# Two graph layers on one core: where the late layers' weights and the filler rows are sent from

## The chip, the core and the metric

The kernel runs on one core of a Trainium2 chip. A core has five engines that each work through their own queue of instructions in order: TensorE (PE, with its weight loads shown as PEld), VectorE (DVE), ScalarE (ACT), GpSimd (POOL) and SyncE (SP). A transfer (DMA) is issued by an instruction in the queue of SyncE, ScalarE or GpSimd. The metric is the device time of one execution in microseconds; lower is better.

## The reference, cut to what matters

Sixteen graphs of 1024 nodes with 64 channels, given as dense 0/1 adjacency matrices, go through two layers. Each layer normalizes, applies a graph network and adds its input back.

```python
def first_network(x, adj, mask, W1, b1, W2, b2):
    # neighbours; of nodes with more than 10, every skip-th edge is removed, both ways
    nb = neigh.sum(-1); skip = where(nb > 10, (nb + 1) // 2, 1)
    rem = neigh & (skip > 1) & (rank % skip == skip - 1) & mask
    nd = adj without (rem | rem.T), with the node itself
    # per node and channel: quantiles 0.25, 0.5, 0.75 over its neighbours' values
    s = sort(where(nd[..., None], x[:, None], inf), axis=2)
    agg = 0.25 * q25(s) + 0.5 * q50(s) + 0.25 * q75(s)
    return (relu((x + agg) @ W1 + b1) @ W2 + b2) * mask

def second_network(x, adj, W1, b1, g1, be1, m1, v1, ..., Wl, bl):
    # three graph convolutions, each with a batch norm of fixed statistics
    x1 = bn(relu(adj @ (x  @ W1) + b1), g1, be1, m1, v1)
    x2 = bn(relu(adj @ (x1 @ W2) + b2), g2, be2, m2, v2)
    x3 = bn(relu(adj @ (x2 @ W3) + b3), g3, be3, m3, v3)
    return relu(concat(x1, x2, x3) @ Wl + bl)

h = maximum(layernorm(x), 0); x = x + first_network(h, adj, mask, ...)
h = maximum(layernorm(x), 0); x = x + second_network(h, adj, ...)
```

## The kernel before

The graphs are handled in eight pairs. Each pair passes three stages.

- `prepare(p)` (L639) makes a pair ready. It loads `x` (L648), normalizes it (L600 to L608), and writes the result to `h_d` (L652) and, in four pieces for each graph, to `rows_d` (L655). Then, for each of the two graphs, `prepare_one` (L765) takes the adjacency in eight tiles of 128 rows. A tile `a` is loaded by SyncE (L775) into one of two buffers; ScalarE makes `edge` from it (L782), VectorE makes `one` (L786), TensorE turns that (L789), and ScalarE stores the turned tile in `edgeT` (L792). When a graph's eight tiles are done, `edgeT` is stored (L797) and its diagonal is cleared (L799). Counting, removing edges, ordering the nodes by degree (`place`, L887) and numbering each node's neighbours follow. Last, the pair's normalized values are loaded again (`h_again`, L695) and split into three parts `hp` (L697 to L700).
- Gathering and sorting. For blocks of nodes of like degree, TensorE collects each node's neighbour values by products with `hp` (L1176), and VectorE runs a sorting network over them (L1092) and sums the quantiles. Nodes of three further blocks are fetched instead by GpSimd, row by row from `rows_d` (L1361). A row number there that stands for "no neighbour" points to one of two filler rows that each graph has at the head of its part of `rows_d`: a row of zeros and a row of a very large value.
- `later` (L1537) runs the rest of the first layer and the second layer for a pair: `first_layer` and `next_layer`. These are the only readers of the weights. They begin while the last pair is being sorted.

Ahead of all that stands a set-up part, which makes constants. GpSimd writes 32 lines `line` by memsets (L528) and sends them into the table `bounds` (L530). ScalarE issues the loads of all weights, biases and batch-norm vectors (helpers `weight`, `column`, `row` and `both`, L536 to L582), and VectorE and ScalarE fold each batch norm into a scale and a shift (L571 to L577). Last, VectorE fills a tile `filler` of two rows (L623, L624), and ScalarE sends it to the sixteen places in `rows_d` (L627). The pool of `filler` is opened after the pool of `line` is closed, and takes the same place in the on-chip memory.

What sets the order of the work: the text of the program gives every instruction its rank and its dependences. When the program is built, each engine's queue is laid out from these ranks and from an estimate of when an instruction is ready, so a queue's order can differ from the text's. On the chip each queue then runs in the order laid. In the main loop over pairs, `weave` mixes steps of the next pair's `prepare` and of the gathers into the sort of the present pair, by hand-set shares (`SHARES`, L33). The first pair has no such cover: `prepare(0)` runs to its end before the first gather.

Of the kernel before, what the change touches and what calls it, by code (L numbers as in the profile page):

```python
# [10 lines left out]
F32 = mybir.dt.float32  # L11
# [13 lines left out]
P = 128  # L25
# [383 lines left out]
def graph_layers_kernel(ctx: ExitStack, tc: tile.TileContext, ins, out: bass.AP):  # L409
# [126 lines left out]
    def weight(name, rows, cols, twice=False):  # L536
        t = const.tile([rows * (1 + twice), cols], F32, name=f"w_{name}")
        for k in range(1 + twice):
            nc.scalar.dma_start(out=t[k * rows : (k + 1) * rows, :], in_=ins[name])
        return t  # L540

    def column(name, rows, twice=False):
        t = const.tile([rows * (1 + twice), 1], F32, name=f"c_{name}")
        for k in range(1 + twice):
            nc.scalar.dma_start(out=t[k * rows : (k + 1) * rows, :], in_=ins[name].rearrange("(p o) -> p o", o=1))
        return t

    def row(name, cols):
        t = const.tile([P, cols], F32, name=f"r_{name}")
        nc.scalar.dma_start(out=t, in_=ins[name].partition_broadcast(P))  # L550
        return t

    def both(t, src):

        nc.vector.memset(t, 0.0)
        for k in range(2):
            half = slice(k * C, (k + 1) * C)
            nc.scalar.dma_start(out=t[half, half], in_=src)


    w1 = weight("L0_gnn_W1", C, HID, True)
    w2 = weight("L0_gnn_W2", HID, C)
    b1 = column("L0_gnn_b1", HID)
    b2 = row("L0_gnn_b2", C)
    layers = []
    for i in (1, 2, 3):
        wl = const.tile([P, P], F32, name=f"wl{i}")
        both(wl, ins[f"L1_gnn_W{i}"])
        bl, g, be, m, v = (column(f"L1_gnn_{k}{i}", C, True) for k in ("b", "g", "be", "m", "v"))
        s = const.tile([P, 1], F32, name=f"bn_s{i}")  # L570
        nc.vector.tensor_scalar(s, v, BN_EPS, None, ALU.add)  # L571
        nc.scalar.activation(s, s, AF.Sqrt)
        nc.vector.reciprocal(s, s)
        nc.vector.tensor_tensor(s, s, g, ALU.mult)

        nc.vector.tensor_tensor(m, m, s, ALU.mult)
        nc.vector.tensor_tensor(be, be, m, ALU.subtract)  # L577
        layers.append((wl, bl, s, be))
    wlast = const.tile([P, 3, P], F32, name="wlast")
    for i in range(3):  # L580
        both(wlast[:, i, :], ins["L1_gnn_Wl"][i * C : (i + 1) * C, :])
    blast = row("L1_gnn_bl", C)  # L582

    biases = {}

# [35 lines left out]
    with tc.tile_pool(name="setup_fill", bufs=1) as setup:  # L621
        filler = setup.tile([2, C], F32, name="filler")
        nc.vector.memset(filler, BIG)  # L623
        nc.vector.memset(filler[:1, :], 0.0)  # L624
        for p in range(NP):
            for x in range(2):
                nc.scalar.dma_start(out=rows_d[p][x * ROWS + ZERO_ROW : x * ROWS + BIG_ROW + 1, :], in_=filler)  # L627

    part_z = {
        MID: const.tile([P, len(TAUS), 1, MW], BF16, name="mid_z"),  # L630
# [8 lines left out]
    def prepare(p, pools):  # L639


        work, keep, ps = pools
        st = Pair()
        st.p = p
        room = work.tile([P, 4, 2, NT, C], F32, tag="stays", name="room")
        xt, h, sq = room[:, 0], room[:, 1], room[:, 2].rearrange("p x t c -> p (x t) c")
        for x in range(2):
            nc.sync.dma_start(out=xt[:, x], in_=rows_of(x_d[2 * p + x]))  # L648
        flat = "p x t c -> p (x t) c"
        layernorm_relu(work, h.rearrange(flat), xt.rearrange(flat), sq, T2)  # L650
        for x in range(2):
            nc.sync.dma_start(out=rows_of(h_d[2 * p + x][:, :]), in_=h[:, x])  # L652
            for t in range(4):
                row0 = x * ROWS + 2 + 256 * t
                nc.sync.dma_start(  # L655
                    out=rows_d[p][row0 : row0 + 256, :].rearrange("(u j) c -> j u c", j=32),
                    in_=h[32 * t : 32 * t + 32, x],
                )
        yield
        st.g = {}  # L660
        st.nvs = keep.tile([P, HELD], BF16, tag="nvs", bufs=2, name="nvs")
        r0 = keep.tile([P, 2, NT, SPLIT], U16, tag="r0", name="r0")
        r1 = keep.tile([P, 2, NT, N - REST], BF16, tag="r1", name="r1")
        st.r = (r0, r1)
        rows = {}
        fetch, find_live = [None] * 2, [None] * 2

        def first_rows():
            rows[0] = fetch[0]()

        for x in range(2):
            fetch[x], find_live[x] = yield from prepare_one(st, x, pools, first_rows if x else None)
        rows[1] = fetch[1]()
        yield
        listed = work.tile([P, 2 * len(NODES) - 1, 256], F32, tag="stays", name="listed")
        st.nodes_nv = keep.tile([P, 2 * len(NODES) - 1], F32, tag="nodes_nv", bufs=2, name="nodes_nv")
        for x in range(2):
            find_live[x] = yield from find_live[x](rows[x], listed)
        yield from list_rows(st, listed, pools)
        for x in range(2):  # L680
            find_live[x]()
            yield


        st.z = keep.tile([P, len(TAUS), HELD], BF16, tag="z", name="z")
        half = work.tile([P, HELD], F32, tag="a", bufs=2, name="half")
        nc.vector.tensor_scalar(half, st.nvs, 0.498, MAGIC, ALU.mult, ALU.add)
        nc.vector.tensor_scalar(half, half, MAGIC, None, ALU.subtract)
        for q, (tau, _) in enumerate(TAUS):
            nc.vector.scalar_tensor_tensor(st.z[:, q, :], st.nvs, -tau, half, ALU.mult, ALU.add)  # L690
        yield

        h = work.tile([P, 2, NT, C], F32, tag="a", bufs=2, name="h_again")
        for x in range(2):
            nc.sync.dma_start(out=h[:, x], in_=rows_of(h_d[2 * p + x][:, :]))  # L695
        st.hp = keep.tile([P, 3, 2, NT, C], BF16, tag="hp", name="hp")
        nc.scalar.copy(st.hp[:, 0], h)  # L697
        nc.vector.tensor_tensor(h, h, st.hp[:, 0], ALU.subtract)
        nc.scalar.copy(st.hp[:, 1], h)
        nc.vector.tensor_tensor(st.hp[:, 2], h, st.hp[:, 1], ALU.subtract)  # L700
        yield
        return st
# [743 lines left out]
    def first_layer(pools, xt, h, agg, mask):  # L1446


        one, ps = pools
        X = xt.shape[2]  # L1450
        nc.vector.tensor_tensor(agg, agg, h, ALU.add)  # L1451
        oT = channels_first(pools, agg, "chan")
        yield
        for x in range(X):
            rows = slice(x * C, (x + 1) * C)
            hT = one.tile([HID, N], F32, tag="hT", name="hT")
            for hf in range(NH):
                sl = slice(hf * HALF, (hf + 1) * HALF)
                pm = ps.tile([HID, HALF], F32, tag="mm", name="pm1")
                nc.tensor.matmul(out=pm, lhsT=w1[rows, :], rhs=oT[rows, sl], start=True, stop=True)  # L1460
                nc.scalar.activation(hT[:, sl], pm, AF.Relu, bias=b1)
            py = ps.tile([P, NT, C], F32, tag="mm", name="py")
            for t in range(NT):
                nc.tensor.matmul(out=py[:, t, :], lhsT=hT[:, t * P : (t + 1) * P], rhs=w2, start=True, stop=True)  # L1464
            nc.vector.tensor_tensor(h[:, :, x, :], py, b2[:, None, :].to_broadcast([P, NT, C]), ALU.add)
            yield
        nc.vector.tensor_tensor(h, h, mask[:, :, :, None].to_broadcast([P, NT, X, C]), ALU.mult)
        nc.vector.tensor_tensor(xt, xt, h, ALU.add)
        flat = "p t x c -> p (t x) c"
        layernorm_relu(one, agg.rearrange(flat), xt.rearrange(flat), h.rearrange(flat), NT * X)  # L1470
        yield
        return channels_first(pools, agg, "chan")

    def next_layer(pools, graphs, adjT, x2, cur):
# [4 lines left out]
        XC = X * C  # L1479
        small = adjT[0].dtype == F8  # L1480
        xs = []
        for i, (wl, bl, s, be) in enumerate(layers):

            if small:
                xw = [one.tile([P, NT, XC], BF16, tag=f"xw{k}", name=f"xw{k}") for k in range(3)]
# [33 lines left out]
        for hf in range(NH):  # L1519
            ts = slice(4 * hf, 4 * hf + 4)  # L1520
            pf = ps.tile([P, 4, X, C], F32, tag="mm", name="pf")
            for t in range(4):
                sl = slice((4 * hf + t) * P, (4 * hf + t + 1) * P)
                for i, xT in enumerate(xs):
                    nc.tensor.matmul(  # L1525
                        out=pf[:, t].rearrange("p x c -> p (x c)"), lhsT=xT[:, sl], rhs=wlast[:XC, i, :XC],
                        start=(i == 0), stop=(i == 2),
                    )
            nc.vector.tensor_tensor(
                res[:, ts], pf, blast[:, None, None, :].to_broadcast([P, 4, X, C]), ALU.add  # L1530
            )
        nc.vector.scalar_tensor_tensor(res, res, 0.0, x2, ALU.max, ALU.add)  # L1532
        for x in range(X):
# [210 lines left out]
    with ExitStack() as stack:  # L1744
# [6 lines left out]
        with ExitStack() as inner:  # L1751
# [3 lines left out]
            )  # L1755
            ahead = Steps(prepare(0, early))
            ahead.rest()
            sts = [ahead.result]
            jobs = iter(NODE_ORDER)

# [131 lines left out]
```

## Time and profile before

| what | value |
|---|---|
| time of the kernel, median of 3 runs | 2845.74 us (2841.83 to 2846.65) |
| the profiled execution's own time | 2855.05 us |
| its span, first to last instruction | 2853.2 us |
| mean granted TensorE clock | 0.869 |
| busy: PE, DVE, ACT, POOL | 75%, 79%, 58%, 48% of the span |
| DMA queues: SyncE's, GpSimd's, ScalarE's | 131.39, 62.23 and 8.09 MB |

The page of the profile gives shares over the whole span, the span in 40 slices of 71.3 us, and the costliest groups of instructions. In a timeline line, the first number is the start, the second the duration, both in us; "ACTq" and "SPq" stand for the queue of an engine when it issues a transfer, and the bracket at the end gives how long the engine stood idle before and what ended that. In a line of one source line's instructions, the three durations are least, median and largest in ns. Line numbers such as L627 are those of the kernel before.

### The profile page before, as it was taken

To read this page: it belongs to the slowest core of one execution; us is meant where nothing else is said; L and a number is where in the kernel's file an instruction comes from. 1 tells how busy PE (TensorE), PEld (TensorE's weight loads), DVE (VectorE), ACT (ScalarE), POOL (GpSimd) and SP (SyncE) were. 2 spreads that over 40 slices of the span, in tenths; PEclk is the share of its full clock that TensorE was granted. 3 is DMA by queue.
4 is the path that set the end of the run, shared out by engine and by line. 5 is a ranking of instruction groups with operands and counts; after the bars stand their busy time and mean duration, and the time that the engine had idled before them with its cause. 6 is when DMAs were issued, how large, how long until landed. Compare 5 with 4: busy or idle time off the path is not lost. (4 is left out here: it accounts for less than half of the span.)

```text
span 2853.2 us, 54558 instructions
## 1 busy us (share of the span) xinstructions
PE 2127.4 (75%) x21226; PEld 1374.2 (48%) x21226; DVE 2259.9 (79%) x5356; ACT 1657.8 (58%) x3324; POOL 1358.7 (48%) x1155
## 2 busy tenths in 40 slices
PE   1567986897798699779855986997588496448768
PEld 0344563564455365545523553665355363234445
DVE  3117999889899989989999999989688486647843
ACT  2686788678677858867773777687423141122222
POOL 5115363475526416443734274175646748862220
PEclk9788997998899799789878997998798798778989
DMA  3303222322422323142431222322310351221221
GB/s 96 109 30 98 80 88 65 104 80 58 107 72 86 81 91 91 46 110 68 98 65 45 82 86 73 112 75 61 80 21 19 74 82 51 42 56 39 48 61 46
DMA packets 261035, 205.27 MB, mean 72 GB/s; under 512 B 217120, under 2 KB 217248, under 8 KB 256672
## 3 DMA queue, kind: packets, MB, share of 16 engines
q1 hardware_dynamic: 165120, 131.39, 15.5%
q0 software_dynamic: 39680, 62.23, 9.1%
q10 hardware_dynamic: 55968, 8.09, 2.1%
q8 instruction: 168, 2.75, 0.4%
q14 instruction: 99, 0.81, 0.1%
HBM read 148.82 MB, written 52.75 MB: 71 GB/s over the span
## 5 line engine op out<-in xcount | busy, mean ns | idle before, releaser
L1361 POOL DMA_INDIRECT g_nodes<-rows_d,rows_listed x744 | 979.2, 1316 | 952.5 <-DVE prod L1104 276.2
L1176 PE MATMUL pg<-s,hp 128*64 128x496 fp8e4 (+5 forms) x8064 | 747.0, 337 | 134.9 <-ACT hp L697 56.1
L1176 PEld LDWEIGHTS <-hp 128*64 128x64 bf16 x8064 | 450.2, 113 | 376.9 <-ACT hp L697 67.2
L1509 PE MATMUL pg<-adjT,xw 128*64 128x512 fp8e4 x2304 | 282.5, 394 | 24.6 <-ACT xw L1498 11.4
L895 POOL DMA_INDIRECT live_d<-edge,place x128 | 178.7, 1396 | 191.1 <-DVE place L887 154.9
L1151 DVE TENSOR_SCALAR s<-r 128x3200 uint16<-128x3200 uint16 (+2 forms) x192 | 199.6, 1049 | 56.9 <-PE pg L1176 56.8
L1554 POOL DMA_INDIRECT agg<-agg_d,place x128 | 134.8, 1053 | 196.4 <-DMA agg_d<-agg_nodes 118.0
L1509 PEld LDWEIGHTS <-xw 128*64 128x64 bf16 x2304 | 135.4, 113 | 154.1 <-issue 22.8
L782 ACT ACTIVATE edge<-a 128x1024 fp8e4<-128x1024 uint32 x128 | 135.8, 1062 | 105.1 <-DMA a<-in_adj 87.2
L1180 ACT ACTIVATE g<-pg 128x400 f32<-128x400 f32 (+3 forms) x168 | 84.3, 502 | 191.1 <-PE pg L1176 161.3
L1092 DVE TENSOR_TENSOR t<-g 128x800 f32<-128x800 f32 (+9 forms) x184 | 168.0, 926 | 5.4 <-ACT g L1180 3.4
L884 ACT ACTIVATE stays<-keys,minus 128x1024 fp8e4<-128x1024 f32 x128 | 143.6, 1122 | 41.7 <-PE keys L876 40.5
L865 ACT ACTIVATE edge<-q,bias 128x1024 fp8e4<-128x1024 f32 x128 | 142.2, 1112 | 41.6 <-PE q L860 41.6
L838 ACT ACTIVATE stays<-cs,back 128x1024 f16<-128x1024 f32 x128 | 139.1, 1114 | 41.5 <-DVE look L819 19.8
L789 PE MATMUL ptE<-ident_h,one 128*128 128x128 bf16 x1024 | 83.4, 232 | 106.1 <-DVE one L786 58.0
L1092 DVE TENSOR_TENSOR g<-t 128x992 f32<-128x992 f32 (+7 forms) x176 | 160.0, 934 | 2.4
L1451 DVE TENSOR_TENSOR agg<-agg,h_late 128x1024 f32<-128x1024 f32 x8 | 9.8, 1224 | 184.1 <-DMA agg<-agg_d,place 184.1
L930 PE MATMUL pt<-ident_h,lp 128*128 128x128 bf16 x1024 | 107.7, 276 | 60.7 <-ACT liveT L933 33.2
L1247 PE MATMUL pg<-s,hp 128*64 128x384 bf16 (+14 forms) x1872 | 149.1, 301 | 2.8 <-DVE s L1216 2.7
L792 ACT ACTIVATE edgeT<-ptE 128x1024 fp8e4<-128x1024 f32 x128 | 130.8, 1033 | 19.9 <-PE ptE L789 19.6
L1513 ACT ACTIVATE xT<-pg,c_L_gnn_b 128x512 f32<-128x512 f32 x48 | 32.9, 686 | 183.9 <-PE pg L1509 175.3
L786 DVE TENSOR_SCALAR one<-a 128x1024 fp8e4<-128x1024 f32 x128 | 88.5, 696 | 55.6 <-DMA a<-in_adj 45.3
(253 smaller groups left out, 5043.3 us busy)
## 6 DMA issues: line engine op xcount, KB each, us to landing
a<-in_adj SPq DMA_DIRECT2D x128, 512.0 KB
adjT_d<-edgeT SPq DMA_DIRECT2D x16, 1024.0 KB
lp<-live_d POOLq DMA_DIRECT2D x32, 512.0 KB
adjT<-adjT_d SPq DMA_DIRECT2D x16, 1024.0 KB
g_nodes<-rows_d,rows_listed POOLq DMA_INDIRECT x744
room<-in_x SPq DMA_DIRECT2D x16, 256.0 KB
h_d<-room SPq DMA_DIRECT2D x16, 256.0 KB
rows_d<-room SPq DMA_DIRECT2D x64, 64.0 KB
```

The costliest lines, as they stand in the source:

```text
L782: nc.scalar.activation(edge[:, t, :], a[:, :].bitcast(U32), AF.Sign, accum_out=found[:, 0, b, t : t + 1], saturate=False)
L838: nc.scalar.activation(stays[:, t, :], cs, AF.Abs, bias=back[:, t : t + 1], scale=2.0)
L865: nc.scalar.activation(edge[:, t, :], q, AF.Relu, bias=bias(-2.0), accum_out=nv[:, t : t + 1], saturate=False)
L884: nc.scalar.activation(junk, keys, AF.Sign, bias=minus[:, t : t + 1], accum_out=above[:, t : t + 1], saturate=False)
L895: sent = nc.gpsimd.indirect_dma_start(out=live_d[b][:, :], out_offset=bass.IndirectOffsetOnAxis(ap=place[:, b, t : t + 1], axis=0), in_=ed ...
L1092: sorted_by[0] = nc.vector.tensor_tensor(view(bufs, o, n1, n2), view(bufs, a, n1, n2), view(bufs, b, n1, n2), ALU.max if op else ALU.min)
L1151: nc.vector.tensor_scalar(s[:, j, :, us, :], st.r[0][:, :, us, j0:j1], abs(k - 3), 0x0808, ALU.logical_shift_right if k > 3 else ALU.logic ...
L1176: summed = nc.tensor.matmul(out=pg[x * C : (x + 1) * C, those, :], lhsT=st.hp[:, part, x, u, :], rhs=picked, start=(i == 0 and part == 0), ...
L1247: summed = nc.tensor.matmul(out=pg[x * C : (x + 1) * C, ks, w0:], lhsT=st.hp[:, part, x, u, :], rhs=s[:, ks, x, u, w0:], start=(whole and ...
L1361: asked = nc.gpsimd.indirect_dma_start(out=g[:, k, a * C : (a + 1) * C], out_offset=None, in_=rows_d[st.p][:, :], in_offset=bass.IndirectO ...
L1509: nc.tensor.matmul(out=pg[cs, :], lhsT=part[:, u, cs], rhs=adjT[x][:, u, sl], start=(u == 0 and k == 0), stop=(u == NT - 1 and k == len(xw ...
L1554: nc.gpsimd.indirect_dma_start(out=agg[:, t, x, :], out_offset=None, in_=agg_d[b][:, :], in_offset=bass.IndirectOffsetOnAxis(ap=place[:, b ...
```

## The change

The loads of weights move from ScalarE to SyncE. They are wrapped in a function `load_weights`, called once after `prepare(0)` has been written out, and each load is ordered behind the latest `h_again` load on SyncE, which at that moment is the first pair's. The order is one of the queue alone: nothing waits for the `h_again` data. The batch-norm steps move into the same function. Their readers take them from an object `weights`. The sixteen sends of filler rows move from ScalarE's queue to GpSimd's. The helper `both` is renamed `blocks_of`.

```diff
     def weight(name, rows, cols, twice=False):
         t = const.tile([rows * (1 + twice), cols], F32, name=f"w_{name}")
         for k in range(1 + twice):
-            nc.scalar.dma_start(out=t[k * rows : (k + 1) * rows, :], in_=ins[name])
+            load_one(t[k * rows : (k + 1) * rows, :], ins[name])
         return t
...
-    w1 = weight("L0_gnn_W1", C, HID, True)
-    w2 = weight("L0_gnn_W2", HID, C)
-    b1 = column("L0_gnn_b1", HID)
-    b2 = row("L0_gnn_b2", C)
-    layers = []
-    for i in (1, 2, 3):
...
+    read_last = [None]
+
+    def load_one(to, source):
+
+        load = nc.sync.dma_start(out=to, in_=source)
+        tc.add_manual_dep(
+            load.ins, read_last[0].ins.name,
+            mybir.DependencyInfo(mybir.DependencyClass.NoSync, mybir.DependencyReason.SCHED_ONLY),
+            reason="weights are wanted late",
+        )
...
+    def load_weights():
+
+        w = weights
+        w.w1 = weight("L0_gnn_W1", C, HID, True)
+        w.w2 = weight("L0_gnn_W2", HID, C)
+        w.b1 = column("L0_gnn_b1", HID)
+        w.b2 = row("L0_gnn_b2", C)
+        w.layers = []
+        for i in (1, 2, 3):
+            wl = const.tile([P, P], F32, name=f"wl{i}")
+            blocks_of(wl, ins[f"L1_gnn_W{i}"])
+            bl, g, be, m, v = (column(f"L1_gnn_{k}{i}", C, True) for k in ("b", "g", "be", "m", "v"))
+            s = const.tile([P, 1], F32, name=f"bn_s{i}")
+            nc.vector.tensor_scalar(s, v, BN_EPS, None, ALU.add)
+            nc.scalar.activation(s, s, AF.Sqrt)
...
+            w.layers.append((wl, bl, s, be))
+        w.wlast = const.tile([P, 3, P], F32, name="wlast")
+        for i in range(3):
+            blocks_of(w.wlast[:, i, :], ins["L1_gnn_Wl"][i * C : (i + 1) * C, :])
+        w.blast = row("L1_gnn_bl", C)
...
-                nc.scalar.dma_start(out=rows_d[p][x * ROWS + ZERO_ROW : x * ROWS + BIG_ROW + 1, :], in_=filler)
+                nc.gpsimd.dma_start(out=rows_d[p][x * ROWS + ZERO_ROW : x * ROWS + BIG_ROW + 1, :], in_=filler)
...
         for x in range(2):
-            nc.sync.dma_start(out=h[:, x], in_=rows_of(h_d[2 * p + x][:, :]))
+            read_last[0] = nc.sync.dma_start(out=h[:, x], in_=rows_of(h_d[2 * p + x][:, :]))
...
             ahead = Steps(prepare(0, early))
             ahead.rest()
+            load_weights()
             sts = [ahead.result]
```

More of the change, by code (lines that the diff above doesn't have):

```diff
@@ L544, in column @@
         for k in range(1 + twice):
-            nc.scalar.dma_start(out=t[k * rows : (k + 1) * rows, :], in_=ins[name].rearrange("(p o) -> p o", o=1))
+            load_one(t[k * rows : (k + 1) * rows, :], ins[name].rearrange("(p o) -> p o", o=1))
         return t
@@ L549, in row, with blocks_of @@
         t = const.tile([P, cols], F32, name=f"r_{name}")
-        nc.scalar.dma_start(out=t, in_=ins[name].partition_broadcast(P))
+        load_one(t, ins[name].partition_broadcast(P))
         return t
-    def both(t, src):
+    def blocks_of(t, src):
         nc.vector.memset(t, 0.0)
@@ L557, in both @@
             half = slice(k * C, (k + 1) * C)
-            nc.scalar.dma_start(out=t[half, half], in_=src)
-    w1 = weight("L0_gnn_W1", C, HID, True)
-    w2 = weight("L0_gnn_W2", HID, C)
-    b1 = column("L0_gnn_b1", HID)
-    b2 = row("L0_gnn_b2", C)
-    layers = []
-    for i in (1, 2, 3):
[L567 to L582, printed above, removed]
+            load_one(t[half, half], src)
+    read_last = [None]
[6 more added lines that the diff above has]
+        )
@@ new lines, in graph_layers_kernel @@
+    class Weights:
+        pass
+    weights = Weights()
+    def load_weights():
[12 more added lines that the diff above has]
+            nc.scalar.activation(s, s, AF.Sqrt)
+            nc.vector.reciprocal(s, s)
+            nc.vector.tensor_tensor(s, s, g, ALU.mult)
+            nc.vector.tensor_tensor(m, m, s, ALU.mult)
+            nc.vector.tensor_tensor(be, be, m, ALU.subtract)
+            w.layers.append((wl, bl, s, be))
[3 more added lines that the diff above has]
+        w.blast = row("L1_gnn_bl", C)
@@ L1459, in first_layer @@
                 pm = ps.tile([HID, HALF], F32, tag="mm", name="pm1")
-                nc.tensor.matmul(out=pm, lhsT=w1[rows, :], rhs=oT[rows, sl], start=True, stop=True)
-                nc.scalar.activation(hT[:, sl], pm, AF.Relu, bias=b1)
+                nc.tensor.matmul(out=pm, lhsT=weights.w1[rows, :], rhs=oT[rows, sl], start=True, stop=True)
+                nc.scalar.activation(hT[:, sl], pm, AF.Relu, bias=weights.b1)
             py = ps.tile([P, NT, C], F32, tag="mm", name="py")
             for t in range(NT):
-                nc.tensor.matmul(out=py[:, t, :], lhsT=hT[:, t * P : (t + 1) * P], rhs=w2, start=True, stop=True)
-            nc.vector.tensor_tensor(h[:, :, x, :], py, b2[:, None, :].to_broadcast([P, NT, C]), ALU.add)
+                nc.tensor.matmul(out=py[:, t, :], lhsT=hT[:, t * P : (t + 1) * P], rhs=weights.w2, start=True, stop=True)
+            nc.vector.tensor_tensor(h[:, :, x, :], py, weights.b2[:, None, :].to_broadcast([P, NT, C]), ALU.add)
             yield
@@ L1481, in next_layer @@
         xs = []
-        for i, (wl, bl, s, be) in enumerate(layers):
+        for i, (wl, bl, s, be) in enumerate(weights.layers):
             if small:
@@ L1525, in next_layer @@
                     nc.tensor.matmul(
-                        out=pf[:, t].rearrange("p x c -> p (x c)"), lhsT=xT[:, sl], rhs=wlast[:XC, i, :XC],
+                        out=pf[:, t].rearrange("p x c -> p (x c)"), lhsT=xT[:, sl], rhs=weights.wlast[:XC, i, :XC],
                         start=(i == 0), stop=(i == 2),
@@ L1529, in next_layer @@
             nc.vector.tensor_tensor(
-                res[:, ts], pf, blast[:, None, None, :].to_broadcast([P, 4, X, C]), ALU.add
+                res[:, ts], pf, weights.blast[:, None, None, :].to_broadcast([P, 4, X, C]), ALU.add
             )
```

## The prediction

> **What bounds the kernel now.** I read the page first, then busy time by stretch over the first 330 us, then the waits of the first 80 us, then the timeline there, and last the durations of single DMA issues. On the page, one digit is a fortieth of the span (71.3 us):
>
> ```profile
> DVE  3117999889899989989999999989688486647843
> ACT  2686788678677858867773777687423141122222
> ```
>
> VectorE (DVE) is nearly full from the fifth slice to the 28th: sorting sets the pace there. In the first 230 us it is nearly empty, because nothing can be sorted before the first pair of graphs is prepared. That stretch is a chain with nothing beside it, so a microsecond saved in it should reach the end whole. All that the change touches stands in this chain or just behind it. Busy time by stretch (first the stretch, its length, then PE, PEld, DVE, ACT, POOL with counts, granted clock, DMA share, GB/s):
>
> ```profile
> 0.00:32.30 32.30, 1.89 (x16) 1.60 (x16) 15.44 (x192) 1.89 (x4) 21.71 (x51) 1.00 0.27 60
> 32.30:44.05 11.75, 2.07 (x16) 1.54 (x16) 4.08 (x5) 9.86 (x18) 9.29 (x25) 1.00 0.73 179
> 44.05:61.10 17.05, 1.89 (x16) 1.62 (x16) 1.46 (x4) 0.00 (x0) 8.60 (x47) 1.00 0.24 66
> 61.10:72.50 11.40, 2.07 (x16) 1.64 (x17) 2.08 (x3) 9.64 (x18) 0.00 (x0) 1.00 0.55 184
> 228.00:262.00 34.00, 26.69 (x318) 17.82 (x320) 19.52 (x23) 24.75 (x65) 26.69 (x25) 0.81 0.58 148
> ```
>
> ScalarE (ACT) does two bursts of four adjacency tiles in 11.75 and 11.40 us, and before each it stands still: 32.3 us with 1.89 busy, and 17.05 us with nothing. The timeline says why:
>
> ```profile
> 31.66 0.59 ACTq L550 DMA_DIRECT2D r_L_gnn_bl<-in_L_gnn_bl  x1
> 33.26 1.04 ACT L782 ACTIVATE edge<-a 128x1024 fp8e4<-128x1024 uint32 x1
> 54.05 0.48 POOL L530 DMA_DIRECT2D bounds<-line  x1 [0.29 <-POOL line L528]
> 55.66 0.11 DVE L623 MEMSET filler<- 2x64 f32 x1 [13.86 <-DMA bounds<-line]
> 56.03 5.05 ACTq L627 DMA_DIRECT2D rows_d<-filler  x16
> 61.13 1.06 ACT L782 ACTIVATE edge<-a 128x1024 fp8e4<-128x1024 uint32 x1 [17.08 <-DMA rows_d<-filler]
> 77.02 0.42 DVE L799 TENSOR_TENSOR edgeT<-edgeT,off_diag 128x256 int32<-128x256 int32 x1 [2.91 <-DMA adjT_d<-edgeT]
> ```
>
> The first stop is the issue of weights up to 32.3. The second has two owners. The filler tile lies where the lines of `bounds` lay, so its memset waits for GpSimd's last line (54.05 and its landing); VectorE stands 13.86 us at it; and ScalarE stands behind 16 filler DMAs that wait for it, then needs 5.05 us to issue them.
>
> **The change part by part.**
>
> *Weights off ScalarE.* 48 DMAs leave its queue (3 of `w_`, 31 columns, 12 half blocks, 2 broadcast rows). One issue:
>
> ```profile
> L545 ACTq DMA_DIRECT2D c_L_gnn_v<-in_L_gnn_v x6: 607/609/612, 9.2 to 27.1; - x6
> L1283 ACTq DMA_DIRECT2D agg_d<-o x112: 308/343/2842, 369.3 to 2600.8; - x112
> L1407 SPq DMA_DIRECT2D agg_d<-agg_nodes x32: 326/388/1597, 328.1 to 2732.9; - x32
> ```
>
> 48 x 0.607 = 29.1 us, nearly all of the first stop. A rule of the Trainium skill speaks against a gain (page "DMA: Bandwidth & Descriptors", section "Issuing engines are not separate DMA queues"): issuing from several engines saves only the time of the issue, usually small beside the transfer. By the rule this part is worth about 0. By the row an issue is 0.607 us for at most 32 KB, and 48 of them stand ahead of the chain's first activation. I go by the row. Without them tile 0, asked for at 5.79, can be taken about 3.6 us later (a tile asked for at 34.42 was taken at 37.99): at 9.4 instead of 33.26. Two tiles come before the normalization, whose own chain (L600 to L608, six VectorE steps and two ScalarE steps, some 7 us) then runs beside the tiles. Eight tiles at 2.5 us, plus 6.4 us in which SyncE writes `h_d` and `rows_d` (37.17 to 43.59) instead of asking for tiles, end near 9.4 + 20 + 6.4 = 36 us; before it was 71.3.
>
> *Filler to GpSimd.* Its issue of a small DMA is 0.48 us (L530), so 16 x 0.48 = 7.7 us, from 56 to 64. GpSimd has nothing from 54.5 to 123.7, and its first reader of the rows is at 227.7: cost nothing, and 7.7 us if that cover were gone. ScalarE no longer waits. The memset stays, though, and still waits for the last line at about 55.7: the lines are GpSimd's own work (82 memsets, 23.6 us, and 32 issues, 15.8 us), which nothing here shortens. What is late next is therefore VectorE, which takes its queue in order: all that is put behind the memset waits to 55.7. Where it is put decides the gain. Queues follow an order made when the program is built, from estimated readiness and not from the text (`one`, L786, ran at 15.75 ahead of L576 at 17.27, written far earlier). Before, the memset was put after the fourth tile, 8.8 to 13.7 us after ScalarE's start at 32.3. ScalarE's start moves some 23 us earlier, so the same moment is 32 to 37 us after the new start: all eight `one` (the last near 33, 24 us after the start) come first, and L799, which waits for the store of the eighth (5.5 us, from 71.5 to 77.0), comes behind. L799 then runs at 55.8 instead of 77.0: **gain 21**. Ends: the memset ahead of the fifth `one` as before gives 5.6 (the fifth and sixth tiles' buffers free at 56.6 instead of 62.2); a memset that holds nothing gives 77.0 - 42 = 35. I take 21, by the order as worked out.
>
> *Weights onto SyncE.* They are put behind the last `h_again` of the first pair. What stands there:
>
> ```profile
> 227.46 0.99 SPq L695 DMA_DIRECT2D h_again<-h_d  x2
> 232.00 0.34 SPq L775 DMA_DIRECT2D a<-in_adj  x1
> 236.16 0.69 DVE L786 TENSOR_SCALAR one<-a 128x1024 fp8e4<-128x1024 f32 x1
> 236.76 1.22 DVE L700 TENSOR_TENSOR hp<-h_again,hp 128x1024 bf16<-128x1024 f32 x1
> 242.17 47.96 SPq L775 DMA_DIRECT2D a<-in_adj  x9
> ```
>
> On SyncE these 48 shapes have no row. Bounds: 0.33 (its tile loads), 15.8 us in all, and 0.607 as on ScalarE, 29.1. The like stores above show SyncE no faster than ScalarE (388 against 343 ns), so 29. All being ready at once and earlier in the text than the second pair, they go ahead of its tiles: a second-pair tile asked for at 232.0 is asked for at 257.6 (times of before), behind it ten `h_d` and `rows_d` writes, then the rest. It can be taken at 261, 25 us late. But the eight `one` of that graph were spread from 236 to 288 by the weaving (SyncE once waited 25.9 us for one of them); from 261, at 2.5 us each and 6.4 for the writes, they end at 287. If the queues are laid with the late loads in mind, almost nothing is lost. The batch-norm steps come along: 15 of VectorE at 0.15 (2.3 us), 3 roots of ScalarE at 0.2, and six memsets. VectorE has 14.5 us and ScalarE 9 us idle in 228 to 262, so they cost 0 if the weights arrive when the queue expects them. Before, VectorE waited 10.0 us in all for `c_v`, mostly with nothing to do, but the first 1.57 us with memsets behind it: an issue takes longer than the order assumed. Such waits now stand before the first gather. I bound the part by 0 and 25 and take **3**. The weights' readers come after 2000 us.
>
> Sum: -21 + 3 = **-18 us**: 2855.05 (the profiled execution; its span 2853.2) becomes 2837. That execution was 9.3 us above the median of 2845.74; the difference is carried over to the median: **2828 us**.
>
> **The rivals.**
>
> *The filler keeps its place (little happens).* If the memset again stands before the fifth `one`, the start gains 5.6 and pays 3: 2843. For it: the order is not in the diff, and 13.86 us of waiting shows that it misjudged the lines once. Against it: eight tiles would be ready well before the moment that it was given. This is also the case in which the change does not free the start as it says.
>
> *The filler falls far back.* If it stands behind L820 or among L839, the chain gains 29 to 35; with 2 or 3 paid, 2813 to 2818. For it: VectorE has little to do there and the order may be late rather than early.
>
> *SyncE's burst holds VectorE (slower).* If the second pair's first `one` keeps its place just before L700, VectorE waits for a tile 25 us late; L700 makes the third part of `hp`, which every gather of the first block reads, so TensorE, and the first sort, wait too: +25. It outweighs the start as soon as that gains less than 25. With a start gain of 14, midway between 5.6 and 21, it gives +11: 2857. For it: the trace has exactly this order, and the row of 29 us. Against it: the loads' lateness is known when the order is made, and the `one` can simply move behind.
>
> **How the numbers follow.** Forecast 0.50 (own range 2818 to 2837), filler far back 0.16, filler in place 0.14, slower 0.20. About 0.2% (5.7 us) is what a measurement of this kernel can tell from no change. The first two are faster beyond it: 0.66; the third lies within it: 0.14; the last is slower: 0.20. The range reaches from 2808, below the far-back case, to 2854, which leaves out the larger half of the slower one.
>
> **What would show it.** ScalarE's first L782 near 9 to 12 us and no stop behind filler; a memset L623 still at about 55.7, with the eighth `one` before and L799 right after it; 16 filler issues of GpSimd between 56 and 64; the first gather (L1176, 233.7 before) near 213; 48 issues of SyncE over 26 to 29 us behind L695; the second pair's `one` starting some 25 us after them with VectorE waiting under 5 us for a tile. Wrong if fewer than six `one` run before the memset, if VectorE or ScalarE waits over 10 us for weights or the second pair's tile, or if the first gather's lead is gone by the first sort's end (293.4 before).

## The result and the profile after

The changed kernel took 2827.78 us (median of 7 runs, 2820.77 to 2834.53) against 2845.74 of the kernel before (7 runs, 2840.51 to 2851.97) on the same chip: ratio 0.9937, 95% interval 0.9918 to 0.9956, which is 18.0 us. The forecast was 2828.0. In a later group of runs, where the changed kernel was measured again beside the last experiments, the ratio was 0.9904 (0.9874 to 0.9934). The profiled execution took 2820.77 us, with a span of 2819.0 us against 2853.2. These two spans differ by 34.2 us, more than the kernels do: 2820.77 is the lowest of its kernel's seven runs, and the profiled 2855.05 of before lies above all seven of its own. So below, places in the first 480 us are compared, not spans. In lines below, numbers such as L805 are those of the changed kernel; they lie 19 or 20 above those of before (L786 has become L805, L623 L642, L799 L818, L819, which makes `look`, L838, L838 L857, L1176 L1195, L627 L646).

The two engine rows of the page, in slices of 70.5 us:

```profile
DVE  3137998999999899989999999999688486647943
ACT  4795877678587768868673777687423141122222
```

ScalarE's first slice has gone from 2 to 4, and VectorE's third (141 to 211 us) from 1 to 3: more of the first pair's preparation and the start of its sort have come forward. From the fourth slice on the rows are nearly those of before. Three of the prediction's stretches (first the stretch and its length, then PE, PEld, DVE, ACT, POOL with counts, clock, DMA share, GB/s):

```profile
0.00:32.30 32.30, 4.99 (x40) 3.94 (x40) 19.15 (x184) 14.55 (x23) 20.41 (x46) 1.00 0.55 147
44.05:61.10 17.05, 4.58 (x37) 2.19 (x37) 1.21 (x9) 3.37 (x7) 12.43 (x58) 1.00 0.23 74
228.00:262.00 34.00, 30.87 (x385) 21.07 (x383) 27.87 (x42) 13.56 (x29) 22.66 (x18) 0.95 0.53 137
```

ScalarE now has 14.55 us of work in the first 32.3 us (1.89 before), and the DMA engines are at 0.55 instead of 0.27. The second of these stretches is still almost empty on every engine but GpSimd: a stop is left there. In the last stretch VectorE does 27.87 us instead of 19.52, because the first pair's sort has begun earlier. The timeline of the start:

```profile
0.76 1.28 ACT L801 ACT_TABLE_LOAD   x1 [0.76 <-PEq L1896]
7.05 1.06 ACT L801 ACTIVATE edge<-a 128x1024 fp8e4<-128x1024 uint32 x1 [5.01 <-DMA a<-in_adj]
37.48 0.69 DVE L805 TENSOR_SCALAR one<-a 128x1024 fp8e4<-128x1024 f32 x1 [1.61 <-DMA a<-in_adj]
46.19 0.42 DVE L818 TENSOR_TENSOR edgeT<-edgeT,off_diag 128x256 int32<-128x256 int32 x1 [2.34 <-DMA adjT_d<-edgeT]
58.48 0.49 POOL L530 DMA_DIRECT2D bounds<-line  x1 [0.29 <-POOL line L528]
60.15 0.11 DVE L642 MEMSET filler<- 2x64 f32 x1 [13.53 <-DMA bounds<-line]
60.37 0.10 DVE L827 COPY nb<-nbp 128x8 f32<-128x8 f32 x1
60.73 8.15 POOL L646 DMA_DIRECT2D rows_d<-filler  x16 [1.76 <-DVE act L831]
61.34 2.20 ACT L857 ACTIVATE stays<-cs,back 128x1024 f16<-128x1024 f32 x2 [10.66 <-DVE look L838]
211.21 0.88 PE L1195 MATMUL pg<-s,hp 128*64 128x400 fp8e4 x4 [9.95 <-DVE ln_var L624]
```

ScalarE takes the first tile at 7.05 instead of 33.26, the eighth `one` runs at 37.48 (68.49 before), and L818 at 46.19 instead of 77.02. VectorE then stands 13.53 us at the memset of the filler, which still waits for GpSimd's last line. ScalarE stands 10.66 us behind that, for `look`. The first `stays` (L857, the first step behind the counting) starts at 61.34; before it was 83.37. The first gather starts at 211.21 instead of 233.66. The two lines of the kernel before:

```profile
83.37 1.11 ACT L838 ACTIVATE stays<-cs,back 128x1024 f16<-128x1024 f32 x1 [1.20 <-PE cs L834]
233.66 0.88 PE L1176 MATMUL pg<-s,hp 128*64 128x400 fp8e4 x4 [10.30 <-ACT hp L697]
```

SyncE's queue behind the first pair:

```profile
205.01 0.99 SPq L714 DMA_DIRECT2D h_again<-h_d  x2
206.06 1.92 SPq L565 DMA_DIRECT2D w_L_gnn_W<-in_L_gnn_W  x3
...
237.23 0.58 SPq L565 DMA_DIRECT2D r_L_gnn_bl<-in_L_gnn_bl  x1
244.57 26.90 SPq L794 DMA_DIRECT2D a<-in_adj  x10
```

The 48 weights take SyncE from 206.06 to 237.81, 31.8 us. The second pair's `h_d` and `rows_d` follow, and its tiles come from 244.57 on. Its first `one` runs at 250.83 (before: 236.16).

### The profile page after: what moved, and what is told of

Same layout as the page of the kernel before. It is cut to its first block, busy times and chain, and to the rows that moved or that the text cites. A ratio compares the mean times of both kernels' runs of the same rounds, so it can differ in the third digit from the quotient of the medians.

```text
span 2819.0 us, 54552 instructions
## 1 busy us (share of the span) xinstructions
PE 2124.0 (75%) x21226; PEld 1366.3 (48%) x21226; DVE 2260.5 (80%) x5356; ACT 1660.1 (59%) x3325; POOL 1359.1 (48%) x1171
## 5 line engine op out<-in xcount | busy, mean ns | idle before, releaser
L1380 POOL DMA_INDIRECT g_nodes<-rows_d,rows_listed x744 | 968.6, 1302 | 951.7 <-DVE prod L1123 282.6
L1195 PE MATMUL pg<-s,hp 128*64 128x496 fp8e4 (+5 forms) x8064 | 742.2, 335 | 128.9 <-ACT hp L716 47.4
L1195 PEld LDWEIGHTS <-hp 128*64 128x64 bf16 x8064 | 445.1, 113 | 370.4 <-ACT hp L716 67.5
L857 ACT ACTIVATE stays<-cs,back 128x1024 f16<-128x1024 f32 x128 | 138.8, 1114 | 47.3 <-DVE look L838 28.7
L805 DVE TENSOR_SCALAR one<-a 128x1024 fp8e4<-128x1024 f32 x128 | 89.5, 704 | 53.9 <-DMA a<-in_adj 42.6
```

The lines of the kernel that those rows point to most:

```text
L857: nc.scalar.activation(stays[:, t, :], cs, AF.Abs, bias=back[:, t : t + 1], scale=2.0)
L1195: summed = nc.tensor.matmul(out=pg[x * C : (x + 1) * C, those, :], lhsT=st.hp[:, part, x, u, :], rhs=picked, start=(i == 0 and part == 0), ...
L1380: asked = nc.gpsimd.indirect_dma_start(out=g[:, k, a * C : (a + 1) * C], out_offset=None, in_=rows_d[st.p][:, :], in_offset=bass.IndirectO ...
```

## The experiments

The variants were run in two groups, each beside the kernel before on one chip. Its median was 2853.59 us beside the first three variants of the table and after_filler_own_place, and 2846.56 beside the other four; the row of the changed kernel is the comparison above. So across the groups only ratios compare. Where an expectation names a time, it reckons from the 2845.74 of the first comparison, and its difference is what counts. This table has the places in the profiles that the verdicts rest on, in us; each comes from one execution:

| kernel | first stays | first gather | second pair's first place | second gather | ratio (95%) |
|---|---|---|---|---|---|
| before | 83.37 | 233.66 | 351.95 | 479.49 | 1 |
| filler_by_GpSimd_alone | 76.22 | 226.86 | 349.15 | 476.69 | 0.9971 (0.9952 to 0.9990) |
| before_filler_own_place | 75.27 | 225.70 | 347.89 | 474.86 | 0.9982 (0.9961 to 1.0004) |
| weights_late_filler_by_ScalarE | 69.28 | 221.69 | 342.65 | 473.58 | 0.9948 (0.9923 to 0.9972) |
| the changed kernel | 61.34 | 211.21 | 331.12 | 458.41 | 0.9937 (0.9918 to 0.9956) |
| after_unchanged | 61.68 | 212.16 | 332.51 | 459.29 | 0.9904 (0.9874 to 0.9934) |
| weights_behind_last_pair | 61.22 | 212.63 | 330.82 | 456.73 | 0.9924 (0.9898 to 0.9951) |
| weights_burst_doubled | 61.25 | 211.40 | 357.56 | 477.65 | 0.9979 (0.9959 to 0.9999) |
| after_filler_own_place | 49.39 | 200.69 | 320.72 | 448.65 | 0.9895 (0.9865 to 0.9926) |
| weights_last_filler_own_place | 48.57 | 199.39 | 318.17 | 447.20 | 0.9880 (0.9846 to 0.9915) |

The row after_unchanged is the changed kernel once more: two executions of one program differ by 0.3 to 1.4 us at these places. The second gather is the start of the second pair's sort. Each variant's queues are laid out anew, so the order of other instructions can differ, too, as it does for after_filler_own_place below.

**Weights moved, filler still sent by ScalarE** (weights_late_filler_by_ScalarE), from the changed kernel:

```diff
-                nc.gpsimd.dma_start(out=rows_d[p][...], in_=filler)
+                nc.scalar.dma_start(out=rows_d[p][...], in_=filler)
```

> The changed kernel, but the filler rows are again sent by ScalarE. The order of VectorE and SyncE is that of the changed kernel. Theory (what holds the start is VectorE's wait at the filler memset, about 60.2 us, and the sender costs its issue and what stands behind it): ScalarE waits for the memset too, sends until about 65.5, and only then makes the sums that VectorE's next step needs; the first stays activation comes at about 67.9 instead of 61.3: 6.5 us slower than the changed kernel, 2834, 11 to 12 faster than before. Rival 1 (the weights alone are the whole gain): 0 to 1 us beside the changed kernel, 2828. Rival 2 (the sender was as much as the weights): the 17 us stop of ScalarE is back, 2845.

Measured: 2836.89 us, 0.9948. The first gather is 12.0 us earlier than before, 10.5 later than with the filler on GpSimd. The timeline says why:

```profile
60.27 0.11 DVE L642 MEMSET filler<- 2x64 f32 x1 [13.38 <-DMA bounds<-line]
60.63 5.02 ACTq L646 DMA_DIRECT2D rows_d<-filler  x16
66.02 1.01 ACT L781 CAST sums<-tot 128x1024 bf16<-128x1024 f32 x1 [21.67 <-DMA rows_d<-filler]
67.50 0.17 DVE L827 COPY nb<-nbp 128x8 f32<-128x8 f32 x1 [6.94 <-PE nbp L823]
```

ScalarE stands 21.67 us, with the sends ahead of `sums` in its queue; TensorE's counting and VectorE's `nb` wait behind it. The first `stays` comes at 69.28 (expected 67.9), 7.9 us later than in the changed kernel. The long stop of ScalarE is back, as the second rival has it, but it costs less than its length, because VectorE is held at the memset until about 60.2 in both kernels. Moving the weights alone gives about half of the start: 12.0 of 22.5 us at the first gather. At the second gather 5.9 of 21.1 are left; what takes the rest was not traced. In whole times, the intervals of this run and of the changed kernel overlap.

**Only the filler moved** (filler_by_GpSimd_alone), from the kernel before:

```diff
-                nc.scalar.dma_start(out=rows_d[p][...], in_=filler)
+                nc.gpsimd.dma_start(out=rows_d[p][...], in_=filler)
```

> The kernel before, with only the sender of the filler rows changed to GpSimd; the order of VectorE, TensorE and SyncE is that of before. Theory: VectorE still stands at the memset to 55.7 ahead of the fifth tile; only the 5.05 us of issue go: 5 to 6 us faster than before, 2840. Rival 2 (the sender was the stop): the 17 us go, 2829. Rival 1 (weights are all): 0, 2846.

Measured: 2843.41 us, 0.9971, which is 8.3 us (interval 2.9 to 13.7; expected 5 to 6). The first gather gains 6.8 us, of which 2.8 is left at the second gather. The memset stays where it was, at 54.85 after 13.41 us of waiting, and VectorE's next `one` with it. ScalarE no longer stops for the sends: it takes two more tiles at 47.11 and 48.40, where before the next came at 61.13, but the weights still hold its first tile. So the parts alone are worth 12.0 and 6.8 at the first gather, and together 22.5: each leaves a part of the other's stop standing.

**The filler in a place of its own** (after_filler_own_place and before_filler_own_place): the tile comes from a pool that shares no space with `line`, so the memset has nothing to wait for. The same edit on each kernel:

```diff
-        filler = setup.tile([2, C], F32, name="filler")
+        filler = const.tile([2, C], F32, name="filler")
```

> The changed kernel, with the filler tile in a place of its own, so that its memset waits for no line. Theory (the memset's wait is what limits the changed kernel's start): VectorE's copy of the neighbour counts follows the sums at about 50 instead of 60.4, the first stays activation at about 51 instead of 61.3: 10 us faster than the changed kernel, about 2817. Rival 3 (the adjacency loads, or the second graph's tiles on ScalarE, bind next): less than 4 us faster, 2824 to 2828.

> The kernel before, with only the filler tile in a place of its own; weights and filler rows are still sent by ScalarE. Theory: the sends follow the weights at once and take 5 us, the 17.05 us stop goes, so the chain gains 12: 2834. Rival 2 (ScalarE's sending is what costs, the place does not matter): 0 to 2 us, 2844 to 2846.

Measured: 2820.38 us, 0.9895, on the changed kernel; 2848.01 us, 0.9982, on the kernel before. The first did what was expected:

```profile
6.70 0.11 DVE L642 MEMSET filler<- 2x64 f32 x1
42.46 0.43 DVE L818 TENSOR_TENSOR edgeT<-edgeT,off_diag 128x256 int32<-128x256 int32 x1 [1.88 <-DMA adjT_d<-edgeT]
```

The first `stays` runs 12.0 us earlier than in the changed kernel, of which 9.8 is left at the second gather. Not all of the 12.0 is the memset: L818 itself ran 3.7 us earlier (42.46 against 46.19), since SyncE asked for six tiles and not four ahead of its writes of `h_d` and `rows_d`, and the eighth turned tile was stored at 36.77 instead of 40.44. From L818 to the first `stays` it took 6.9 us instead of 15.2, and these 8.2 us are the memset's stop. The second missed its expectation of 2834: by the ratio it gains 5.1 us, and its interval, 0.9961 to 1.0004, does not exclude that it gains nothing. The memset ran early (14.11), but the sends moved, too:

```profile
14.11 0.11 DVE L623 MEMSET filler<- 2x64 f32 x1
32.28 5.88 ACTq L627 DMA_DIRECT2D rows_d<-filler  x16
39.17 1.04 ACT L782 ACTIVATE edge<-a 128x1024 fp8e4<-128x1024 uint32 x1
```

Now they stand right behind the weights (whose last issue ends at 32.24) and ahead of the first tile, which ScalarE takes at 39.17 instead of 33.26. It gained 8.1 us at the first `stays`, where the 17 us stop, less 5 us for the sends, had been expected to give 12. The sends cost 5.9 us ahead of the first tile, and where the stop had been ScalarE now stands 3.4 us for the load of the fifth tile (at 53.96).

**The burst of weights put elsewhere** (weights_behind_last_pair): `load_weights()` is called when the last pair has been prepared.

```diff
             ahead.rest()
-            load_weights()
...
+                if p == NP - 2:
+                    load_weights()
```

> The weights' 48 loads are issued by SyncE only behind the last pair's preparation instead of behind the first's. The theory, that the burst behind the first pair costs about 3 us net: second pair's first 'one' again ahead of the first gather, first block's aggregation at about 271 instead of 273.7, time 2 to 3 us under the changed kernel's (ratio about 0.992). Rival, the burst is fully hidden: same time within 1 us. Rival, the burst holds VectorE: 8 us or more under.

Measured: 2826.55 us, 0.9924, against 0.9904 of the changed kernel beside it. The expected gain of 2 to 3 us isn't seen in the time, which is 5.1 us longer, with overlapping intervals. In the profile it is there, if one counts from the first gather of the same execution: the first block's aggregation, the end of the first sort, starts 59.6 us behind it without the burst (272.24 against 212.63; in the kernel before 59.7), and 62.5 and 63.0 us behind it in the two profiles with the burst. So the burst costs about 3 us there. The second pair's tiles show how the rest was absorbed. Their first `one` ran at 215.1 without the burst and at 250.8 with it, but the first `stays` of that pair started at almost one time. In the timeline of weights_behind_last_pair:

```profile
283.01 2.12 ACT L857 ACTIVATE stays<-cs,back 128x1024 f16<-128x1024 f32 x2 [3.56 <-DVE look L838]
```

In that of the changed kernel:

```profile
285.06 2.10 ACT L857 ACTIVATE stays<-cs,back 128x1024 f16<-128x1024 f32 x2
```

Without the burst, the `one` of that graph's eight tiles are spread from 215 to 267, and three of them run before VectorE's first sorting step; with it all eight are packed between the sorting steps from 250.8 to 270.7. So a burst of 31.8 us moves the `stays` by 2.1 us, or by 3.5 counted from the first gather.

**The burst doubled** (weights_burst_doubled):

```diff
+            twin = const.tile([P, 24], F32, name="twin")
+            for k in range(48):
+                load_one(twin[k % 2 * C : k % 2 * C + C, k // 2 : k // 2 + 1], ins["L1_gnn_v1"]...)
```

> 48 further small loads (64 partitions by one number, into a tile that nobody reads) are issued by SyncE right behind the 48 weights, which makes the burst about 61 us long. Theory, hidden mostly by the work on tiles already there: second pair's first 'one' about 29 us later (near 280), time 3 to 10 us above the changed kernel's. Rival, free: 0 to 2 us. Rival, SyncE's burst holds VectorE one for one: 29 us above.

Measured: 2842.64 us, 0.9979, which is 21.2 us above the changed kernel of its group, with intervals that don't meet. The theory's 3 to 10 is refuted, and neither rival's number fits. The added loads took 32.62 us of SyncE. Of its timeline, with the second pair's first `stays`:

```profile
238.49 32.62 SPq L565 DMA_DIRECT2D twin<-in_L_gnn_v  x48
276.76 24.30 SPq L794 DMA_DIRECT2D a<-in_adj  x10
315.05 2.12 ACT L857 ACTIVATE stays<-cs,back 128x1024 f16<-128x1024 f32 x2 [0.30 <-DVE look L838]
```

The second pair's first `stays` moved by 30.0 us (from 285.06 in the changed kernel), its first `place` by 26.4 and the second gather by 19.2. VectorE was not held one for one at the tile (it stood 4.34 us for the first, at 280.79): the first block's aggregation of the first pair was even earlier (266.95 against 273.74), as no `one` now runs ahead of it. It lost work later, 6.0 us from 270 to 300 us, around the late tiles, and 7.6 us from 340 to 370. Busy time in the latter stretch of the changed kernel (columns as above):

```profile
340.00:370.00 30.00, 29.09 (x348) 19.27 (x346) 26.11 (x74) 23.42 (x42) 23.70 (x17) 1.00 0.26 83
```

and with the burst doubled:

```profile
340.00:370.00 30.00, 24.99 (x301) 17.71 (x303) 18.49 (x56) 27.52 (x57) 19.45 (x18) 0.89 0.50 150
```

VectorE's work falls from 26.11 to 18.49 us there, with ScalarE nearly full (27.52 of 30 us) and the DMA engines at 0.50 instead of 0.26: the second pair's tiles come in this stretch now (six `one` instead of one). Which of its waits holds the sort is not separated. So the first 31.8 us of burst moved the second pair by 2.1, the next 32.6 by 30.0: the cover of this place is just about used up by the weights themselves.

**The changed kernel unchanged**, as the baseline of this group:

> The changed kernel itself, so that the three beside it can be compared with it on the same chip. Ratio to before 0.992 to 0.995, first stays activation near 61.3, first gather near 211, first block's aggregation near 274.

Measured: 2821.46 us. The places came as expected (61.68, 212.16 and 275.12), but the ratio of 0.9904 lies below the expected 0.992 to 0.995. Its interval and the one of the first comparison share only 0.9918 to 0.9934, so the gain in time is known no better than to some 7 us: 18.0 in one pair of medians, 25.1 in the other.

**Both gains together** (weights_last_filler_own_place): the edits of weights_behind_last_pair and of after_filler_own_place.

> As weights_behind_last_pair, and the filler rows have a place of their own on the chip, so that their memset waits for no bounds line. Theory: the two gains add, first stays near 49.4, first gather near 198 to 201, first block's aggregation near 261, ratio 0.988 to 0.989. Rival, the second gain is lost again in the sort that follows: ratio as with the filler's own place alone or above (0.9895).

Measured: 2816.16 us, 0.9880 (0.9846 to 0.9915), the best of all, and below both kernels. The first gather is 34.3 us ahead of before, the second 32.3. From weights_behind_last_pair, run beside it, it differs by the filler's place alone: the medians are 10.4 us apart (2816.16 against 2826.55), and the intervals of the ratios overlap a little (0.9898 to 0.9915). Against after_filler_own_place (0.9895) the difference is well inside the intervals. So the filler's place is the gain that these runs support; that the weights' later place adds to it is not shown.

## Why the prediction was right, point by point

- *Weights off ScalarE: right.* Its first tile came at 7.05 (forecast 9.4), the eighth `one` at 37.48 ("near 33"), and the eighth turned tile was stored at 40.3 (36). The start was better, as SyncE asked for the first tile at 2.95 instead of 5.79, and the pace worse than worked out: VectorE took the first `one` only at 14.07, with the normalization's steps ahead of it, though ScalarE had been done with two tiles at 9.4. The moment of the last tile comes out within 5 us because the two errors go opposite ways.
- *Filler to GpSimd, cost nothing: right.* The 16 sends took 8.15 us from 60.73 (forecast 7.7 from 56), with GpSimd free. That ScalarE no longer waits is worth 8 us at the first `stays`, 10.5 at the first gather: the row weights_late_filler_by_ScalarE against the changed kernel.
- *The memset decides: right in kind, wrong in two details that cancel, which is luck.* It was forecast at 55.7, with L818 (L799) right behind it at 55.8. It ran at 60.15, since the lines themselves ended 4.4 us later (58.48 against 54.05), and it stood one step further back, between L818 and L827, with TensorE's and ScalarE's counting behind L818 (46.19 to 50.1) already done. The late lines cost 4.4 us and the counting already done saved about 5 (6.35 us from L799 to `stays` before, 1.2 from the memset to `stays` now). So the first `stays` gained 22.0 us, forecast 21. What the memset still costs is shown by after_filler_own_place: 8.2 us of the 12.0 gained there.
- *Weights onto SyncE, 3 us: right in size, close to a cliff.* 31.8 us of issue (forecast 29), the first `one` 39.6 us behind the first gather instead of 2.5; cost about 3 us at the end of the first sort. Counted from the first gather, the first tile was asked for 35.0 us later than before (33.4 us behind it instead of 1.7 ahead), where 25.6 had been worked out: SyncE wrote the ten pieces of `h_d` and `rows_d` (237.91 to 244.53) ahead of it and not behind it. The cover took this, too. The wait of 25.9 us that the prediction gives for these tiles is the first pair's, between 80 and 150 us; the longest for the second pair's was 20.3. Undone, the burst brought nothing that the time shows. The bound of 0 to 25 was the honest one: the same length again cost 21 us. The weights' own waits (10.0 us in all at L590, three of them, the longest 4.23) cost next to nothing: VectorE's first sorting step starts 26.9 us behind the first gather (238.06), and 26.6 without the weights there (weights_behind_last_pair, 239.24).
- *The sum of 18: borne out, by a route that the profiles allow to check.* 22.5 us at the first gather, 21.1 at the second, 18.0 in the medians of the first comparison and 25.1 in those of the second. That the first median met the forecast to 0.2 us is luck: its interval is some 11 us wide. The prediction's number fits the first interval and lies just outside the second.
- *The rivals.* That the filler keeps its place (gain 5.6) is refuted by the timeline. That it falls far back, worth 2813 to 2818 (its own terms reach to 2820), didn't happen. With the memset out of the way in after_filler_own_place the chain came out as worked out for it: L818 ran at 42.46 (42 forecast), the first `stays` gains 34.0 us (29 to 35 forecast), and 0.9895 of 2845.74 is 2815.9. The slower rival, a burst that holds VectorE, didn't happen; doubling the burst gave a loss of its size by a neighbouring path: not the `one` held before `hp`, but the second pair ready too late.

The rule that the prediction takes from the Trainium skill (page "DMA: Bandwidth & Descriptors", section "Issuing engines are not separate DMA queues") says that the choice of issuing engine saves only the time of the issue, and that this is usually small beside the transfer. The first half agrees with this case, where the time of the issue is what was moved. The second half gives the wrong size here: 48 issues at the head of a chain with no cover were worth 12.0 us at the first gather alone, and with the 16 others 22.5.

## What to carry to other kernels

When issues of transfers stand at the head of a chain with nothing beside it, count each one by the trace and move them to a queue that has slack; then look for what stops the chain next, because two stops at one place are worth more together than alone. Slack has an end: here one burst of 31.8 us was absorbed and the next of 32.6 cost 21, so a cost of nearly nothing says little about the double. A two-row tile that shares space with an earlier buffer held an engine for 13.5 us here. Giving it its own place put the first `stays` 12.0 us earlier in the changed kernel, but only 8.1 in the kernel before, where its sends then stood in front of the first tile: look where the work goes that was freed.

## What had not been expected of the hardware

- A second load of ScalarE's table of functions: before, one (14.14, for the batch norms' root); after, one at 0.76 and one at 17.02, each 1.28 us. The first function wanted is now that of `edge`, not the root. The second stands in the chain's first part:

```profile
17.02 1.28 ACT L625 ACT_TABLE_LOAD   x1
```

- GpSimd's lines ended 4.4 us later although nothing of theirs was changed: 58.48 here and 58.60 in weights_late_filler_by_ScalarE, where tiles are taken from 7 us on; 54.05 and 53.23 (filler_by_GpSimd_alone) where weights come first. GpSimd had begun 1.1 us later (9.52 against 8.45, behind VectorE's `number`); its 82 memsets took 24.95 us instead of 23.58 and the 32 sends 16.99 instead of 15.80. Its waits for the landing of its own lines were nearly the same in sum (6.6 us against 6.3). Beside this ran more work than before: the DMA share of the first 32.3 us was 0.55 instead of 0.27, and VectorE was busy for 19.15 us instead of 15.44. No run here separates the cause.
- An issue of a small weight costs SyncE what it cost ScalarE: median 594 to 598 ns for the columns, against 607 to 609. GpSimd's sends took 0.51 us each.
